# Even superblocks, earlier weight loads, and a PSUM bank for edge weights and sums in a two-layer typed graph transformer

## The chip, the cores and the metric

The kernel runs on one core of one Trainium2 chip. The core has five engines with a queue of instructions each: TensorE (PE, matmuls and transposes by matmul), VectorE (DVE), ScalarE (ACT), GpSimd (POOL) and SyncE (SP), and DMA engines that they feed. The metric is the time of one execution in microseconds (us) on the device.

## The reference, cut to what matters

There are 6,250 nodes with 128 features and 16 types, and 100,000 edges with 32 types, sorted by destination. Each of two layers does:

```python
k = typed_linear(x, ntype, Wk).reshape(n, H, HS)      # H = 8 heads of HS = 16
q = typed_linear(x, ntype, Wq).reshape(n, H, HS)
v = typed_linear(x, ntype, Wv).reshape(n, H, HS)
kT = jnp.einsum('nhd,htdo->nhto', k, Watt)            # every node under every edge type
vT = jnp.einsum('nhd,htdo->nhto', v, Wmsg)
kw = kT[src, :, etype]
m = vT[src, :, etype]
a = jnp.einsum('ehd,ehd->eh', kw, q[dst]) * pri[:, etype].T / SQRT_D
att = edge_softmax(a, dst, n)
hag = jax.ops.segment_sum((m * att[:, :, None]).reshape(-1, H * HS), dst, num_segments=n)
h = jax.nn.silu(typed_linear(hag, ntype, Wa))
alpha = jax.nn.sigmoid(skip[ntype])[:, None]
h = layernorm(h * alpha + x * (1.0 - alpha)) * g + b  # per node
```

Behind the second layer come a linear map (`ff_w`, `ff_b`), the addition of the input and one more layernorm.

## The kernel before

**Tables and gathers.** For every node and every edge type a row of 256 numbers (the key and the value under that edge type) is computed and written to a table in DRAM, one table for each layer (`tabs[0]`, `tabs[1]`). An edge then needs one row of 1 KB, found by its source and type. The nodes are sorted into 49 blocks of 128. Four classes of 11 blocks hold nodes of four types each; five more blocks are mixed and hold any of the 16 types. Within a class the blocks are ordered by degree, and each block has a fixed number of edge slots per node (`OWN_SLOTS` is 25, 21, 19, 18, 17, 16, 15, 15, 14, 12, 11 in each class; the mixed blocks have 28, 20, 16, 14 and 9 gathers). For a slot POOL issues one indirect DMA that gathers 128 rows, one to a partition (L1434), into a buffer `kv` that holds four slots and has 12 copies. Two small memsets into `pause` (L1440) follow every gather on POOL.

**Stages.** From 0 to about 594 us nodes and edges are sorted and the first table is written (98 scatters, L1128). Layer 0 gathers from it until 1888 us. Layer 1 gathers from 1958 to 3106 us, and the last nodes' results leave until 3150 us.

**Superblocks.** Node work is done on superblocks of up to `SB` = 4 consecutive blocks (list `sbs`), 128 to 512 nodes that stand along the free dimension of a tile. The order of the superblocks is the order of the edge work. Before the change a class is cut into its last 3 blocks, its middle 4 and its first 4 by number of blocks alone, and run in the order first, middle, last (83, 63 and 37 slots); mixed superblocks (2 blocks with 48 slots, 3 with 39) follow the first and the second class, and the last class is run as 37, 63, 37 and 46 slots, the last two being pairs of blocks.

**Edge work of a block** (function `edges`). For each buffer of four slots (a chunk), DVE multiplies the keys with the query (L1454, `kv<-kv,q`) and reduces them to one number per slot and head (L1460, `a<-kv`). When a block's gathers are in, the generator `finished` takes over: mask, maximum `m`, difference, exp on ACT, `den` (the sum of the exps), then for each chunk the product of values and weights (`kv<-kv,a`; into `acc` for the first chunk) and the sum into `acc` (`acc<-kv,acc`), and last `sums`, the reduction of the four slots of `acc`. Its instructions go through a recorder, so that all of them have the line L247. In layer 0 weights lie in `a` and sums in `acc`, both in SBUF. In layer 1 the query, the weights and the sums lie in a pair of PSUM banks from the pool `tps` (tile `tb`). One block, `TOP`, has slots for nodes of high degree beside its own; its weights and sums are in SBUF in both layers.

**Node work of a superblock** (generator `nodes`). Sums divided by `den` are transposed (`nb<-ident,hag`), and a typed linear map follows: for each type DVE makes a masked copy `xm` of the transposed features (`xm<-ntb,nb`, or `xm<-ntb,h` where the features have been copied to SBUF first), and PE adds its product with the type's weights in a PSUM bank. Silu, the residual and the layernorm come next. In layer 0 the chain goes on with keys, values and query of the next layer (`wkqv`, outputs `kvT0`, `kvT1` and `qT`, copied out of PSUM by ACT). Then `pieces_of` makes the superblock's part of the second table: for each block and each half of the edge types, matmuls with the edge-type weights `bdk` and `bdv` (L312), copies on ACT (L320, a few on DVE, L318) into `st`, and, eight steps later (`late`, `later`), a scatter on POOL (L1672). In layer 1 the chain ends with the output, scattered by POOL at L1704. The next superblock's query (`queries0`) is made in layer 0 by the same kind of typed map with `wq0`.

**PSUM.** Eight banks: `nps` has two for the node chain (all tiles named `nb`), `tps` three pairs (`tb`).

**What sets the order.** POOL issues in the order in which the code is written. The code is written chunk by chunk, and after each part of a chunk `tick` takes steps of the node work (`work`) and of the table (`pieces`). `spread(work, gen, steps, slots)` says over how many slots so many steps are spread. For the node chain the steps are 33 in layer 0 and 42 in layer 1, more for mixed superblocks (75 in layer 0), and the slots come from `pace`. On DVE, ACT and PE a scheduler orders the instructions, under order dependences that the recorder (`Held`, `stream`) adds so that node work isn't issued sooner than where it was written.

**Start.** `load_later` queues, on SP, the loads of `wq0` and `wa` (1 MB each, L212 and L213), and two memsets on DVE (L511) hold these loads back. DVE scales the keys' edge weights `bdk` by `prit` (L198, L199) before the first table can be computed; SP loads `bdv` and `prit`, ACT loads `bdk`, `Wk` and `Wv`.

## Time and profile before

| what | value |
|---|---|
| median of 3 runs | 3147.55 us (3146.17 to 3155.6) |
| profiled execution | 3152.49 us, span 3150.6 us |
| busy PE / DVE / ACT / POOL | 1561.5 / 1871.8 / 964.4 / 2376.3 us |
| share of the span | 50% / 59% / 31% / 75% |
| gathers of both layers (L1434) | 1,638, mean 998 ns |
| scatters of the second table (L1672) | 98, mean 1062 ns |
| last layer-0 gather to first layer-1 gather | 1887.97 to 1958.36 us |

POOL has the largest share of the span. A row of a view of groups gives busy time and mean, then the engine's idle time ahead of such instructions with what ended it; in the view of waits the columns are total us, times, and the longest. "issue" is idle time in which no wait shows. A window's row gives its length, the busy time of each engine named with its instructions, the granted clock of PE, the share of the 16 DMA engines and GB/s.

### The profile page before, as it was taken

The page shows a single profiled execution, that of the slowest core. Times are in us where ns is not written, and L with a number is a line of the kernel's source. Part 1 is how long each engine was busy: PE and PEld are TensorE (multiplying, and loading weights), DVE is VectorE, ACT ScalarE, POOL GpSimd, SP SyncE. Part 2 cuts the span into 40 slices and gives each one's busy share as a digit, 9 for nine tenths or more (in the row PEclk, how much of TensorE's full clock was granted, in tenths as well). Part 3 has the DMA queues.
Part 4 walks back from the last instruction along what each step waited for, and adds up shares of the span by engine and source line. Part 5 has one row for each costly group of instructions (what it writes and reads, how often), then busy time and mean ns, then how long its engine had stood idle before and what let it go on. Part 6 is the DMA issues. An engine that isn't in the chain of part 4 may idle for free.

```text
span 3150.6 us, 24725 instructions
## 1 busy us (share of the span) xinstructions
PE 1561.5 (50%) x5295; PEld 706.2 (22%) x5295; DVE 1871.8 (59%) x4322; ACT 964.4 (31%) x1599; POOL 2376.3 (75%) x5392
## 2 busy tenths in 40 slices
PE   5999887303675647776688775011221122112112
PEld 2445334101232312332233232000110011001001
DVE  7477655266646656666665553466556675666565
ACT  3887433101444123533354453001100121012111
POOL 3332665588868887888888882888788888888884
PEclk9899766556677767777777686555555556555555
DMA  7999999933777457775688888333333333333331
GB/s 214 421 419 414 390 388 399 299 94 101 256 262 274 157 194 262 279 295 195 233 306 297 304 290 313 104 109 107 99 102 103 110 114 106 100 108 108 98 97 46
DMA packets 174584, 674.80 MB, mean 214 GB/s; under 512 B 52972, under 2 KB 89998, under 8 KB 149374
## 3 DMA queue, kind: packets, MB, share of 16 engines
q0 software_dynamic: 113152, 635.19, 56.1%
q1 hardware_dynamic: 45170, 30.78, 3.4%
q10 hardware_dynamic: 16096, 7.10, 0.9%
q8 instruction: 46, 0.75, 0.1%
q14 instruction: 120, 0.98, 0.1%
HBM read 248.64 MB, written 425.02 MB: 214 GB/s over the span
## 4 chain that ended last, share of the span: by engine, by line
POOL 46%; issue 11%; DMA 10%; DVE 8%; PE 5%; ACT 2%; POOLq 0%; DVEq 0%; ACTq 0%
POOL kv L1434 35%; DMA kv<-tab,ell 9%; POOL pause L1440 7%; PE nb L247 3%; POOL tab L1672 1%; DMA tab<-st,row 1%; DVE kv L1454 1%; POOL out_dram L1704 1%; PE tb L312 1%; DVE kv L247 1%; DVE hs L247 1%; DVE a L1460 1%; DVE acc L247 1%; ACT L247 1%; ACT st L320 1%
## 5 line engine op out<-in xcount | busy, mean ns | idle before, releaser
L1434 POOL DMA_INDIRECT kv<-tab,ell x1638 | 1634.1, 998 | 325.6 <-issue 250.0
L320 ACT COPY st<-tb 128x512 f32<-128x512 f32 (+1 forms) x984 | 677.5, 778 | 555.6 <-PE tb L312 330.4
L1454 DVE TENSOR_TENSOR kv<-kv,tb 128x512 f32<-128x512 f32 (+3 forms) x223 | 143.0, 641 | 449.0 <-DMA kv<-tab,ell 443.6
L1454 DVE TENSOR_TENSOR kv<-kv,q 128x512 f32<-128x512 f32 (+3 forms) x223 | 143.6, 645 | 410.5 <-DMA kv<-tab,ell 404.1
L247 PE MATMUL nb<-ident,hag 128*128 128x128 f32 x98 | 27.1, 417 | 722.2 <-DVE hag L247 722.1
L1440 POOL MEMSET pause<- 128x32 bf16 x3276 | 334.2, 142 | 0.7
L312 PE MATMUL tb<-bdv,kvT 32*128 32x512 f32 x784 | 259.4, 799 | 52.3 <-ACT st L320 51.7
L312 PE MATMUL tb<-bdv,vT 32*128 32x512 f32 x784 | 260.2, 784 | 48.8 <-ACT st L320 45.0
L1460 DVE TENSOR_REDUCE a<-kv 128x32 f32<-128x512 f32 (+2 forms) x446 | 281.5, 634 | 1.2
L1128 POOL DMA_INDIRECT tab<-st,rows x98 | 101.6, 1037 | 199.5 <-ACT st L320 165.3
L247 PE MATMUL nb<-xm,wa 128*128 128x512 f32 (+2 forms) x336 | 187.3, 715 | 106.0 <-DVE xm L247 105.8
L312 PE MATMUL tb<-bdk,kvT 32*128 32x512 f32 x784 | 231.9, 776 | 14.1 <-ACT st L320 13.7
L247 PE MATMUL nb<-xm,wkqv 128*128 128x384 f32 (+2 forms) x504 | 209.5, 579 | 20.8 <-DVE xm L247 20.8
L318 DVE COPY st<-tb 128x512 f32<-128x512 f32 (+1 forms) x192 | 128.7, 708 | 147.6 <-PE tb L312 78.3
L312 PE MATMUL tb<-bdk,kT 32*128 32x512 f32 x784 | 206.0, 783 | 6.5 <-issue 5.8
L247 PEld LDWEIGHTS nb<-ident,hag 128*128 128x128 f32 x98 | 16.1, 205 | 740.5 <-issue 510.5
L247 DVE SCALAR_TENSOR_TENSOR xm<-ntb,nb 128x512 f32<-128x512 bf16 (+2 forms) x304 | 155.3, 562 | 40.0 <-PE nb L247 39.8
L247 PE MATMUL nb<-xm,wq 128*128 128x384 f32 (+2 forms) x168 | 88.5, 678 | 163.4 <-DVE xm L247 163.4
L1672 POOL DMA_INDIRECT tab<-st,row x98 | 104.1, 1062 | 83.7 <-ACT st L320 59.9
L247 PEld LDWEIGHTS nb<-xm,wkqv 128*128 128x128 f32 x504 | 111.7, 228 | 126.0 <-issue 45.5
L247 DVE TENSOR_TENSOR tb<-kv,tb 128x512 f32<-128x512 f32 (+3 forms) x216 | 138.6, 642 | 0.2
L247 PE MATMUL nb<-ident,hs 128*128 128x128 f32 x98 | 33.5, 469 | 205.6 <-DVE hs L247 198.4
(342 smaller groups left out, 2467.8 us busy)
## 6 DMA issues: line engine op xcount, KB each, us to landing
kv<-tab,ell POOLq DMA_INDIRECT x1638
hr<-xrd SPq DMA_DIRECT2D x14, 256.0 KB
hqd<-hs SPq DMA_DIRECT2D x7, 512.0 KB, 3.1
hq<-hqd SPq DMA_DIRECT2D x7, 512.0 KB
xrd<-xr SPq DMA_DIRECT2D x10, 256.0 KB, 23.2
hr<-xrd SPq DMA_DIRECT2D x10, 192.0 KB, 2.8
hqd<-hs SPq DMA_DIRECT2D x5, 384.0 KB
hq<-hqd SPq DMA_DIRECT2D x5, 384.0 KB, 3.2
```

The costliest lines, as they stand in the source:

```text
L247: put = issue(*args, **kwargs)
L312: stream[nc.tensor] = nc.tensor.matmul(pt[:, b], yT[s, i * P:(i + 1) * P], bd[s, tt, :], start=True, stop=True)
L318: nc.vector.tensor_copy(to, pt)
L320: stream[nc.scalar] = nc.scalar.copy(to, pt)
L1128: put = nc.gpsimd.indirect_dma_start(out=tabs[0].rearrange("(n t) c -> n (t c)", t=16), out_offset=bass.IndirectOffsetOnAxis(ap=rows1[:, t ...
L1434: get = nc.gpsimd.indirect_dma_start(out=kv[:, j - j0, :], out_offset=None, in_=tabs[l][:], in_offset=bass.IndirectOffsetOnAxis(ap=ell[:, ...
L1440: nc.gpsimd.memset(pause[:, at % PAUSES, half], 0.0)
L1454: stream[nc.vector] = nc.vector.tensor_tensor(kk, kk, of.unsqueeze(1).to_broadcast([P, c, D]), op=ALU.mult)
L1460: nc.vector.tensor_reduce(to, kk.rearrange("p k (h d) -> p k h d", h=H), axis=AX.X, op=ALU.add)
L1672: put = nc.gpsimd.indirect_dma_start(out=tabs[1].rearrange("(n t) c -> n (t c)", t=16), out_offset=bass.IndirectOffsetOnAxis(ap=row2[:, tg ...
L1704: put = nc.gpsimd.indirect_dma_start(out=out, out_offset=bass.IndirectOffsetOnAxis(ap=node[:, b:b + 1], axis=0), in_=o[:, i, :], in_offset ...
```

## The change

1. The loads of `wq0` and `wa` go to SP directly behind the load of the edge types; the two memsets on DVE that held them go away.
2. Superblocks of a class are cut so that the largest number of slots is as small as can be: `superblocks_of_slots` gives blocks 0 to 2 (65 slots), 3 to 6 (66) and 7 to 10 (52), run in the order 66, 52, 65; the last class is run as blocks 7 to 10 (52), 4 to 6 (48), and then the two pairs of 37 and 46 slots that it ended with before (its first two superblocks had 37 and 63).
3. The slots over which node work is spread come from `room` and `asking` instead of `pace`, mixed superblocks have 91 steps in layer 0 instead of 75, and the table pieces of the last four superblocks are spread over one slot less.
4. In layer 0 a block's weights and sums lie in one PSUM bank (`hold`), sums two slots wide instead of four. A chunk's product is one instruction as before (two in the first chunk), its sum two instructions of 256 numbers a partition. `TOP` keeps SBUF.
5. That bank comes from `nps`, which has one bank left. `linear_of` asks for its output only when the masked copies are made, since features and output share the bank; with 16 types it first copies the features to SBUF (`h2`). The `wkqv` maps of a mixed superblock run in three passes, one for each output, instead of two, and for the other superblocks the matmuls of an output are issued two types at a time.

Core of the diff:

```diff
     def load_later():
-        nc.sync.dma_start(wq0, Wq[0].rearrange("t d o -> d t o"))
-        nc.sync.dma_start(wa, Wa[0].rearrange("t d o -> d t o"))
...
     nc.sync.dma_start(eti, etype)
+    nc.sync.dma_start(wq0, Wq[0].rearrange("t d o -> d t o"))
+    nc.sync.dma_start(wa, Wa[0].rearrange("t d o -> d t o"))
...
-    for w in (wq0, wa):
-        nc.vector.memset(w[:, 0, 0:1], 0.0)
...
+    def linear_of(pool, nps, types, ntb, hT, n, w):
+        types = list(types)
+        if len(types) > TC:
+            h2 = pool.tile([P, SB * P], F32, name="h2", tag="hb")
+            on.scalar.copy(h2[:, :n], hT[:, :n])
+            yield
+            hT = h2
+        some, ps = 2 if len(types) > TC else TC, None
+        for t0 in range(0, len(types), some):
+            xms = list(masked(pool, types[t0:t0 + some], ntb, hT, n))
+            yield
+            if ps is None:
+                ps = nps.tile([P, SB * P], F32, name="nb")
+            for t, xm in xms:
+                on.tensor.matmul(ps[:, :n], w[:, t, :], xm[:, :n],
+                                 start=(t == types[0]), stop=(t == types[-1]))
+            if t != types[-1]:
+                yield
+        return ps
...
-        nps = ctx2.enter_context(tc.tile_pool(name="nps", bufs=2 if fast else 5, space=PSUM))
+        nps = ctx2.enter_context(tc.tile_pool(name="nps", bufs=1 if fast else 5, space=PSUM))
+        hold_ps = ctx2.enter_context(tc.tile_pool(name="hold", bufs=1, space=PSUM)) if fast else None
...
+            evenly = sorted(superblocks_of_slots(OWN_SLOTS),
+                            key=lambda at: sum(OWN_SLOTS[at[0]:at[0] + at[1]]))
             for c in range(NC):
-                cut = [(CB - i0 - k, k) for i0, k in reversed(list(superblocks(CB)))]
+                cut = [evenly[-1], *evenly[:-1]]
                 if c == NC - 1:
-                    cut = [(CB - i0 - k, k) for i0, k in superblocks(CB - SB)]
+                    cut = [(i0 + SB, k) for i0, k in
+                           reversed(superblocks_of_slots(OWN_SLOTS[SB:]))]
                     cut += [(i0, 2) for i0 in range(SB - 2, -1, -2)]
...
                 w = av
-                if l and rest is None:
-                    w = pair[:, 1, D:D + K * H].rearrange("p (k h) -> p k h", h=H)
+                if rest is None:
+                    if l == 0:
+                        held = hold_ps.tile([P, SB * P], F32, name="hold")
+                    w = (pair[:, 1, D:D + K * H] if l else held[:, 2 * D:2 * D + K * H]).rearrange(
+                        "p (k h) -> p k h", h=H)
                 on.scalar.activation(w, av, AF.Exp)
...
-                if l == 0 or rest is not None:
+                if rest is not None:
                     acc = ep.tile([P, CH, D], F32, name="acc", bufs=1)
+                elif l:
+                    acc = pair[:, 0].rearrange("p (k c) -> p k c", k=CH)
                 else:
-                    acc = pair[:, 0].rearrange("p (k c) -> p k c", k=CH)
+                    acc = held[:, :2 * D].rearrange("p (k c) -> p k c", k=2)
+                wide = acc.shape[1]
...
-                    if j > 1:
+                    if j:
                         j0, j1 = chunks[j - 1]
-                        on.vector.tensor_tensor(acc[:, :j1 - j0], kvt[j - 1][:, :j1 - j0, D:],
-                                                acc[:, :j1 - j0], op=ALU.add)
+                        for c0 in range(0 if j > 1 else wide, j1 - j0, wide):
+                            c = min(wide, j1 - j0 - c0)
+                            on.vector.tensor_tensor(acc[:, :c], kvt[j - 1][:, c0:c0 + c, D:],
+                                                    acc[:, :c], op=ALU.add)
...
-                           (42 if l else 33) + (0 if len(sbs[s][2]) == TC else 14 if l else 42),
-                           pace(s + 1) * (1.0 if l or mixed(s) else 0.75))
+                           (42 if l else 33) + (0 if len(sbs[s][2]) == TC else 14 if l else 58),
+                           room(s))
...
+            def asking(s):
+                if l == 0 and mixed(s + 1):
+                    return 26
+                return 0.5 * GB[sbs[s][0]]
+
+            def room(s):
+                then = min(s + 1, len(sbs) - 1)
+                if l or mixed(s):
+                    return slots(then) - 0.5 * GB[sbs[then][0]]
+                if s + 2 >= len(sbs):
+                    return 0.75 * (slots(then) - 0.5 * GB[sbs[then][0]])
+                return slots(then) - max(18, asking(then)) + 8
...
-                    for js in ((0, 1), (2,)):
+                    for j in range(3):
...
                             on.tensor.matmul(ps[:, :n], wkqv[:, j, t, :], xm[:, :n],
                                              start=(t == types[0]), stop=(t == types[-1]))
-                        yield
+                            if t % 2:
+                                yield
```

Where the instructions stand on the engines, before and after:

On SP at the start of the program, before the change; names are the tiles above, and a row's bracket names the counters that it waits for (`DMAHW` are those of DMA lanes that SP and ACT share):

```order
L341 DMA eti<-in_edge_type_dram 128x782
L191 DMA bdv<-in_L_gnn_Wmsg_dram 16x32x16 [waits DVE_49]
L193 DMA prit<-in_L_gnn_pri_dram 16x32 [waits DMAHW0_49]
...
L720 DMA kvs<-kvi 128x782 [waits DMAHW0_49,DVE_49]
L212 DMA wq_90<-in_L_gnn_Wq_dram 128x16x128 [waits DMAHW1_49]
L213 DMA wa<-in_L_gnn_Wa_dram 128x16x128 [waits DMAHW2_49]
```

and after it:

```order
L380 DMA eti<-in_edge_type_dram 128x782
L381 DMA wq_90<-in_L_gnn_Wq_dram 128x16x128
L382 DMA wa<-in_L_gnn_Wa_dram 128x16x128 [waits DMAHW1_49]
L191 DMA bdv<-in_L_gnn_Wmsg_dram 16x32x16 [waits DMAHW4_49,DVE_49]
L193 DMA prit<-in_L_gnn_pri_dram 16x32 [waits DMAHW6_49]
```

Both weight loads stand ahead of the `bdv` and `prit` loads instead of behind them and behind the store of `kvs`.

On DVE in layer 0, where one of the first blocks is finished, before the change:

```order
L247 TENSOR_REDUCE den<-a 128x8 [waits Activation_49]
L247 TENSOR_TENSOR acc<-kv,a 128x512
L247 TENSOR_TENSOR kv<-kv,a 128x4x128
L1460 TENSOR_REDUCE a<-kv 128x32 [waits DVE_49]
L247 TENSOR_TENSOR kv<-kv,a 128x4x128
L247 TENSOR_TENSOR acc<-kv,acc 128x512 [waits DVE_49]
```

and after it (the recorder's line is now L264), with the end of that block and the start of the next one's sums:

```order
L264 TENSOR_REDUCE den<-hold 128x8 [waits Activation_49]
L1530 TENSOR_REDUCE a<-kv 128x32 [waits DVE_49]
L264 TENSOR_TENSOR hold<-kv,hold 128x256 [waits DVE_49]
L1524 TENSOR_TENSOR kv<-kv,q 128x4x128 [waits DMASW2_49,DMASW7_49,DMASW1_49,DMASW0_49]
L264 TENSOR_TENSOR kv<-kv,hold 128x2x128 [waits DVE_49]
...
L264 TENSOR_REDUCE sums<-hold 128x128 [waits DVE_49]
L1524 TENSOR_TENSOR kv<-kv,q 128x4x128 [waits DMASW2_49,DMASW3_49,DMASW1_49,DMASW0_49]
L264 TENSOR_REDUCE den<-hold 128x8 [waits Activation_49]
```

Weights and sums are read from `hold`, the first chunk's product is cut in two, and between one block's `sums` and the next one's `den`, for which ACT must have written the bank anew, stands one product with the query.

On PE in layer 0, at the first superblock's maps to keys, values and query and the first table matmuls, before the change:

```order
L247 MATMUL nb<-xm,wkqv 128x512 [waits DMAHW1_49,DVE_49]
...
L247 MATMUL nb<-xm,wkqv 128x512 [waits DMAHW0_49,PE_49]
...
L247 MATMUL nb<-xm,wkqv 128x512 [waits DMAHW2_49,Activation_49]
...
L312 MATMUL tb<-bdk,kvT_6679 128x512 [waits DMAHW6_49,DMAHW3_49]
L247 MATMUL nb<-ident,qT 128x128 [waits Activation_49]
```

and after it:

```order
L264 MATMUL nb<-xm,wkqv 128x512 [waits DMAHW1_49,DVE_49,PE_49]
...
L264 MATMUL nb<-xm,wkqv 128x512 [waits DMAHW0_49,Activation_49]
...
L351 MATMUL tb<-bdk,kvT_6637 128x512 [waits DMAHW6_49,DMAHW3_49]
L264 MATMUL nb<-xm,wkqv 128x512 [waits DMAHW2_49,Activation_49]
...
L351 MATMUL tb<-bdk,kvT_6637 128x512 [waits DMAHW4_49,DMAHW1_49]
L264 MATMUL nb<-ident,qT 128x128 [waits Activation_49]
```

The second output's matmuls now wait for ACT's copy too, and a table matmul stands between the second and the third.

60 lines of the change are left out of this document (36 added, 24 removed).

## The prediction

> **What bounds the kernel now.** I read the page's first parts, then the waits of POOL, then POOL's gathers by layer, and last what stands beside a slow gather. Columns of a timeline row: start, duration, engine, line, operation, tiles, and in brackets the idle time before it with what ended it.
>
> ```profile
> span 3150.6 us, 24725 instructions
> POOL 3332665588868887888888882888788888888884
> POOL 46%; issue 11%; DMA 10%; DVE 8%; PE 5%; ACT 2%; POOLq 0%; DVEq 0%; ACTq 0%
> ```
>
> From slice 9 to the end POOL is busy 8 tenths, and the chain that ended last is mostly POOL. POOL issues the 1,638 gathers (L1434), two pacing memsets (L1440) behind each, and the scatters of the second table (L1672). What remains idle in a slot is a fixed 0.15 us of issue, so a slot lasts 0.95 + 0.15 + 0.20 + about 0.01 us = 1.31 us and the layers last as long as POOL's queue. A microsecond counts if POOL stops for it, or if a gather itself takes longer. Both are visible in layer 0:
>
> ```profile
> 594.00:1990.00 1396.00, 871.30 (x844) 0.72 0.68 239
> 1990.00:3106.00 1116.00, 762.77 (x795) 0.54 0.35 104
> L1434 POOL DMA_INDIRECT kv<-tab,ell x844: 952/952/3714, 594.1 to 1989.8; - x169
> L1434 POOL DMA_INDIRECT kv<-tab,ell x795: 951/952/2406, 1989.8 to 3104.8; - x199
> ```
>
> Rows 1 and 2 are POOL's busy time in gathers by window, rows 3 and 4 their minimum, median and maximum in ns. Median 952 in both layers, yet layer 0 has 871.30 - 844 x 0.952 = 67.8 us above it, layer 1 only 762.77 - 795 x 0.952 = 5.9. The layers do the same gathers; they differ in where DVE's operands lie. Layer 0 keeps weights (a) and sums (acc) in SBUF, layer 1 in PSUM (tb). Beside the slowest gather:
>
> ```profile
> 1145.99 0.68 DVE L1454 TENSOR_TENSOR kv<-kv,q 128x512 f32<-128x512 f32 x1
> 1146.17 1.93 POOL L1434 DMA_INDIRECT kv<-tab,ell  x1 [0.15 <-issue]
> 1148.39 0.68 DVE L247 TENSOR_TENSOR acc<-kv,acc 128x512 f32<-128x512 f32 x1
> 1148.45 3.71 POOL L1434 DMA_INDIRECT kv<-tab,ell  x1 [0.15 <-issue]
> 1148.99 0.68 DVE L247 TENSOR_TENSOR kv<-kv,a 128x512 f32<-128x512 f32 x1
> 1150.66 0.68 DVE L247 TENSOR_TENSOR acc<-kv,acc 128x512 f32<-128x512 f32 x1
> 1152.52 0.95 POOL L1434 DMA_INDIRECT kv<-tab,ell  x1 [0.15 <-issue]
> 1885.22 1.44 POOL L1434 DMA_INDIRECT kv<-tab,ell  x1 [0.15 <-issue]
> 1415.56 2.18 POOL L1434 DMA_INDIRECT kv<-tab,ell  x1 [0.15 <-DMA tab<-st,row]
> ```
>
> The gather of 1148.45 lasts until DVE's run of products and sums with two SBUF inputs is over. I laid each of layer 0's 189 gathers above 1.00 us beside the DVE instructions it overlaps: 118 (the first at 643.88 with 1.00 us, the last at 1885.22) overlap a product with a or a sum into acc, 45.5 us above the median; 17 overlap mostly xm<-ntb,h, which also reads twice from SBUF (1415.56 is one), 5.3 us; the remaining 54 overlap kv<-kv,q and others, 15.3 us.
>
> The second loss is POOL standing still:
>
> ```profile
> POOL tab L1672 <- ACT st L320: 59.9, 10, 22.7
> POOL kv L1434 <- DVE acc L247: 20.6, 9, 11.6
> 879.71 1.01 POOL L1672 DMA_INDIRECT tab<-st,row  x1 [8.05 <-ACT st L320]
> 942.54 1.18 POOL L1434 DMA_INDIRECT kv<-tab,ell  x1 [11.56 <-DVE acc L247]
> 1234.47 1.01 POOL L1672 DMA_INDIRECT tab<-st,row  x1 [4.88 <-ACT st L320]
> 1261.91 1.48 POOL L1672 DMA_INDIRECT tab<-st,row  x1 [8.50 <-ACT st L320]
> ```
>
> Those four amount to 33.0 us in the middle of layer 0. Behind the one of 942.54 stands a long piece of PE:
>
> ```profile
> 929.46 7.61 PE L247 MATMUL nb<-xm,wkqv 128*128 128x384 f32 x21
> 940.38 0.51 ACT L247 ACTIVATE a<-a 128x336 f32<-128x336 f32 x1
> 940.92 0.76 DVE L247 TENSOR_REDUCE den<-a 128x8 f32<-128x336 f32 x1 [7.71 <-ACT a L247]
> ```
>
> ACT's exp stands in its queue behind copies of PE's outputs; DVE waits 7.71 us for it, the 12 gather buffers stay full, POOL waits 11.56.
>
> **The change part by part.**
>
> *Weight loads earlier.* Two 1 MB loads leave the middle of the preparation:
>
> ```profile
> 36.14 0.85 SPq L212 DMA_DIRECT2D wq<-in_L_gnn_Wq_dram  x1
> 37.45 2.68 SPq L213 DMA_DIRECT2D wa<-in_L_gnn_Wa_dram  x1
> 40.00:44.00 4.00, 0.16 (x1) 0.00 (x0) 0.00 (x0) 0.30 (x2) 0.45 (x1) 1.00 1.05 300
> 45.92 2.04 PE L312 MATMUL tb<-bdk,kT 32*128 32x512 f32 x5 [5.76 <-issue]
> ```
>
> From 40 to 44 us the DMA engines are full (share 1.05) while PE does 0.16 us, and the first table matmul starts 5.76 us late. Without the loads I take -4.5, some of the wait being the node-row gathers'. They now go ahead of the bdv and prit loads, which shift back; two memsets vanish, and the loads take other DMA lanes, on which bdk's loads wait. If prit, which DVE needs, comes later than that wait saved, the end is +4; if all goes, -7.
>
> *Weights and sums in PSUM.* The 118 gathers' cause goes, except in the one block with overflow edges (SBUF still) and beside what is left in SBUF: 45.5 - 4.5 = -41. Ends: 0 (kv<-kv,q takes the place) and -45.5. DVE pays:
>
> ```profile
> L247 DVE TENSOR_TENSOR kv<-kv,a 128x512 f32<-128x512 f32 x135 | 90.9, 683 | 0.0
> L247 DVE TENSOR_TENSOR kv<-kv,tb 128x512 f32<-128x512 f32 x130 | 86.2, 678 | 0.1
> L247 DVE TENSOR_TENSOR acc<-kv,acc 128x256 f32<-128x256 f32 x10 | 4.2, 417 | 0.0
> L247 DVE TENSOR_REDUCE sums<-acc 128x128 f32<-128x512 f32 x49 | 50.7, 1034 | 0.0
> L247 DVE SCALAR_TENSOR_TENSOR xm<-ntb,h 128x384 f32<-128x384 bf16 x32 | 16.7, 554 | 3.2 <-PE nb L247 2.7 <-ACT h L247 0.3
> 594.00:1958.00 1364.00, 865.97 (x2710) 363.37 (x2710) 813.74 (x1758) 492.34 (x663) 1116.93 (x2555) 0.72 0.68 242
> 1360.00:1440.00 80.00, 65.40 (x197) 29.91 (x197) 59.30 (x126) 23.63 (x34) 70.66 (x156) 0.83 0.63 225
> ```
>
> The product costs the same (678 against 683 ns). The sum is two instructions of 256 wide: 2 x 417 - 684 = 150 ns more for each of 135 + 49 chunks (the first chunk's product is also cut in two), 27 us; the reduction reads 256 instead of 512, about half of 1034, -25. Estimate +2 to +20 us of DVE in all. The third window column is DVE: 813.74 of 1364 us, 60%, so this hides; if it did not, it would be the +20. A new wait: the bank is one, so exp of a block waits until the block before is reduced, and behind it in ACT's queue wait table copies, behind den the sums. At most a copy and an exp, about 1.5 us, 48 times, on DVE's idle 550 us: nothing. [...]
>
> *One bank for the node chain.* In the two superblocks of all 16 types, xm now reads h2 from SBUF everywhere: from 64 such instructions in layer 0 to 160 (query 32, after-attention 32, and wkqv in three passes instead of two, 96), at 5.3 / 64 = 0.083 us of gather each: 96 x 0.083 = +8. In layer 1, 32 more: +2.7. Ends: 0 and double. The added pass is 32 xm x about 0.5 = 16 us of DVE, 8 in each mixed stretch: 59.30 becomes some 70 of 80 us, still under POOL's pace. PE waits at each wkqv output until ACT has copied the one before: a copy as short as exp's 0.51 and what is queued ahead of it. I allow 2.4 us a wait, under a third of the 7.71 that den waited for ACT's queue, three times a chain, 7 us. Scatters are issued 8 steps late (about 12 slots of 1.31 us, 16 us), which absorbs it. At a layer's end nothing does, but ACT's queue is short there: one such wait, +2.4 in layer 0 and +2 in layer 1.
>
> *Even superblocks and the planner's numbers.* Largest superblock 83 slots before, 66 after; node work is told to use more of the superblock behind it (58 steps instead of 42 for mixed), and the matmuls of 4 types come two at a time, so exp stands behind less. I take off 23 of the 33.0 us; all or nothing are the ends, and as much as 22 can come anew in the mixed stretches.
>
> *End of layer 0.*
>
> ```profile
> 1888.34 1.02 POOL L1672 DMA_INDIRECT tab<-st,row  x1 [0.17 <-issue]
> 1933.10 0.97 POOL L1672 DMA_INDIRECT tab<-st,row  x1 [22.72 <-ACT st L320]
> 1958.36 0.99 POOL L1434 DMA_INDIRECT kv<-tab,ell  x1 [11.99 <-DMA tab<-st,row]
> ```
>
> From the last gather (1887.97) to layer 1 are 70 us, its chain: finish, node chain, table, landing. The last superblock is the same two blocks; the order shows 8 scatters behind the last gather instead of 10, -2, against the +2.4: 0.
>
> **Sum.** -4.5 - 41 + 8 - 23 + 0 + 2.7 + 2 = -55.8. The profiled execution took 3152.49 us (1.9 around its span), 4.9 above the median of 3147.55; the difference is set against the median: 3092. 0.3% is 9.4 us, about what a measurement of this kernel can tell from no change.
>
> **The rivals.**
>
> *Stalls stay or move.* The gathers are cured but the mixed stretches fill DVE, and exp still stands behind copies. For it: 59.30 of 80 us already, more work there. Against: longer room for the node work. Without the 23: 3115; with 20 new: 3135.
>
> *kv<-kv,q takes the place.* It keeps two SBUF inputs:
>
> ```profile
> L1454 DVE TENSOR_TENSOR kv<-kv,q 128x512 f32<-128x512 f32 x184 | 127.0, 691 | 369.8 <-DMA kv<-tab,ell 364.8 <-issue 4.7
> ```
>
> For it: 15.3 us are beside it and others today. Against: it comes singly, paced by landings (its idle time, 369.8 us, ends with DMA), and has 127.0 us beside the others' 215 or so (products 90.9, as many sums of 684 ns, 49 first products), but at most 15.3 us of the excess beside their 45.5. Half the gain lost: 3113.
>
> *Operands aren't the cause.* Then only DVE's run, not its inputs, holds POOL: none of -41 + 8, so 3125. Against: layer 1 runs the same sequence from PSUM with 5.9 us. [...]
>
> *Slower: the one bank.* PE is in order; a matmul that waits for ACT's copy holds table matmuls queued behind it, ACT holds exp, and POOL the scatter. It decides when a chain is late by the 16 us of slack and 4.7 more in each of the 14 node chains (66 us, to above 3157). Against: the three waits make 7 us.
>
> **Chances.** Forecast 0.55 (alone 3075 to 3108), stalls 0.20, kv<-kv,q 0.09, operands 0.05, the one bank 0.11. Of the stalls and operands 0.04 ends within 9.4 us of before, of the bank 0.01; so faster 0.85, same 0.05, slower 0.10. Low: everything gone, -7 - 45.5 + 5 - 33 = -80, with the +4.7, 3070, some lower for fewer stalls in layer 1 (3063); high 3138 takes in the first three rivals.
>
> **What would show it.** Right: some 840 us instead of 871.30 for layer 0's 844 gathers, median 952; the four waits under 10 us together; PE's idle before the first table matmul near 1 us; xm<-ntb,h 160 in layer 0, slow gathers only there. Wrong: gathers' total unchanged, POOL waiting for DVE's hold or st in the mixed stretches, PE idle at nb released by ACT with scatters late behind.

## The result, and the profile after

The changed kernel takes 3120.59 us (median of 4 runs, 3117.41 to 3121.85), the kernel before 3151.57 us (4 runs). The ratio is 0.9891 with a 95% interval of 0.9871 to 0.9912: 1.1% faster, some 31 us where 56 were forecast.

The profiled execution took 3117.41 us. From the page of the changed kernel, the span, POOL in 40 slices, and the chain that ended last by engine:

```profile
span 3115.6 us, 25058 instructions
POOL 3332665488888888888888864888788888888884
POOL 41%; DVE 11%; issue 10%; DMA 10%; PE 6%; ACT 2%; POOLq 0%; DVEq 0%; ACTq 0%
```

POOL still sets the pace; the dip in slices 24 and 25 is the stretch between the layers. Its gathers (now L1504), layer 0's 819 by window and by minimum, median and maximum, then layer 1's 819:

```profile
594.00:1843.00 1249.00, 805.28 (x819) 0.75 0.70 247
L1504 POOL DMA_INDIRECT kv<-tab,ell x819: 952/952/3987, 594.7 to 1841.4; - x164
L1504 POOL DMA_INDIRECT kv<-tab,ell x819: 951/952/4115, 1916.3 to 3068.1; - x164
```

For the same 819 gathers the kernel before has these rows:

```profile
594.00:1890.00 1296.00, 848.22 (x819) 0.73 0.68 237
L1434 POOL DMA_INDIRECT kv<-tab,ell x819: 952/952/3714, 594.1 to 1887.0; - x164
L1434 POOL DMA_INDIRECT kv<-tab,ell x819: 951/952/2406, 1958.4 to 3104.8; - x164
```

The median gather is unchanged and layer 0's are 42.9 us shorter in sum: the excess over 952 ns fell from 68.5 to 25.6 us. First and last start in these rows cut the span into five stretches:

| stretch (us) | before | after | difference |
|---|---|---|---|
| up to the first gather of layer 0 | 594.1 | 594.7 | +0.6 |
| first to last gather of layer 0 | 1292.9 | 1246.7 | -46.2 |
| last gather of layer 0 to first of layer 1 | 71.4 | 74.9 | +3.5 |
| first to last gather of layer 1 | 1146.4 | 1151.8 | +5.4 |
| from there to the end | 45.8 | 47.5 | +1.7 |

Everything gained lies in layer 0's gathering, and the other four stretches give back 11 us. POOL's longest stops in layer 0, the counterparts of the four of before:

```profile
791.33 1.14 POOL L1740 DMA_INDIRECT tab<-st,row  x1 [3.56 <-ACT st L359]
924.54 1.25 POOL L1504 DMA_INDIRECT kv<-tab,ell  x1 [6.70 <-DVE t L264]
1153.55 1.31 POOL L1740 DMA_INDIRECT tab<-st,row  x1 [5.17 <-ACT st L359]
1329.98 1.16 POOL L1740 DMA_INDIRECT tab<-st,row  x1 [3.58 <-ACT hold L264]
```

They are shorter but more: ten stops of over 1 us with 28.2 us in all, against four with 33.0. The one at 924.54 stands at the block with overflow edges (`TOP`), as the one of 11.56 us at 942.54 did before. DVE's groups in layer 0 that answer to those shown of before:

```profile
L264 DVE TENSOR_TENSOR hold<-kv,hold 128x256 f32<-128x256 f32 x381 | 160.7, 422 | 3.8
L264 DVE TENSOR_TENSOR kv<-kv,hold 128x512 f32<-128x512 f32 x130 | 88.4, 680 | 1.0
L264 DVE SCALAR_TENSOR_TENSOR xm<-ntb,h 128x384 f32<-128x384 bf16 x80 | 42.3, 553 | 11.3 <-PE nb L264 6.6 <-ACT h L264 3.9
L264 DVE TENSOR_REDUCE sums<-hold 128x128 f32<-128x256 f32 x48 | 19.9, 415 | 0.5
594.00:1916.00 1322.00, 843.11 (x2710) 350.10 (x2710) 837.84 (x2032) 492.99 (x660) 1072.65 (x2555) 0.75 0.70 249
```

The last row is the window of layer 0 up to layer 1 (third column DVE): 837.84 us instead of 813.74, in 42 us less.

### The profile page after: what moved, and what is told of

It reads as the page before. It is cut to its first block, busy times and chain, and to the rows that moved or that the text cites. A ratio compares the mean times of both kernels' runs of the same rounds, so it can differ in the third digit from the quotient of the medians.

```text
span 3115.6 us, 25058 instructions
## 1 busy us (share of the span) xinstructions
PE 1542.5 (50%) x5295; PEld 692.5 (22%) x5295; DVE 1896.9 (61%) x4594; ACT 966.2 (31%) x1605; POOL 2335.1 (75%) x5392
## 4 chain that ended last, share of the span: by engine, by line
POOL 41%; DVE 11%; issue 10%; DMA 10%; PE 6%; ACT 2%; POOLq 0%; DVEq 0%; ACTq 0%
POOL kv L1504 32%; DMA kv<-tab,ell 8%; POOL pause L1510 7%; PE nb L264 5%; DMA tab<-st,row 2%; DVE xm L264 2%; PE tb L351 2%; DVE kv L264 1%; DVE kv L1524 1%; POOL out_dram L1772 1%; DVE hold L264 1%; DVE hs L264 1%; DVE a L1530 1%; POOL tab L1740 1%; ACT L264 1%
## 5 line engine op out<-in xcount | busy, mean ns | idle before, releaser
L1504 POOL DMA_INDIRECT kv<-tab,ell x1638 | 1593.7, 973 | 324.7 <-issue 247.2
L264 PE MATMUL nb<-ident,hag 128*128 128x128 f32 x98 | 26.2, 406 | 641.7 <-DVE hag L264 613.1
L1530 DVE TENSOR_REDUCE a<-kv 128x32 f32<-128x512 f32 (+3 forms) x446 | 281.3, 633 | 1.3
L264 PE MATMUL nb<-xm,wa 128*128 128x384 f32 (+2 forms) x336 | 188.8, 726 | 150.1 <-DVE xm L264 145.2
L264 PE MATMUL nb<-xm,wkqv 128*128 128x384 f32 (+2 forms) x504 | 217.9, 582 | 55.1 <-DVE xm L264 44.3
L351 PE MATMUL tb<-bdv,kvT 32*128 32x512 f32 x784 | 223.2, 749 | 42.5 <-ACT st L359 42.1
L351 PE MATMUL tb<-bdk,kT 32*128 32x512 f32 x784 | 212.3, 809 | 1.9 <-DMA kvs<-kvi 1.9
L264 DVE TENSOR_TENSOR hold<-kv,hold 128x256 f32<-128x256 f32 (+1 forms) x410 | 169.1, 412 | 4.2
L264 PEld LDWEIGHTS nb<-ident,hag 128*128 128x128 f32 x98 | 15.5, 200 | 660.8 <-issue 459.5
L264 PE MATMUL nb<-xm,wq 128*128 128x384 f32 (+2 forms) x168 | 87.0, 672 | 136.3 <-DVE xm L264 130.2
L264 PEld LDWEIGHTS nb<-xm,wa 128*128 128x128 f32 x336 | 89.6, 283 | 250.5 <-issue 190.5
L264 PEld LDWEIGHTS nb<-xm,wkqv 128*128 128x128 f32 x504 | 106.0, 223 | 175.8 <-issue 94.5
L264 DVE TENSOR_TENSOR tb<-kv,tb 128x512 f32<-128x512 f32 (+3 forms) x216 | 138.5, 641 | 0.2
```

The costliest lines, as they stand in the source:

```text
L264: put = issue(*args, **kwargs)
L351: stream[nc.tensor] = nc.tensor.matmul(pt[:, b], yT[s, i * P:(i + 1) * P], bd[s, tt, :], start=True, stop=True)
L1504: get = nc.gpsimd.indirect_dma_start(out=kv[:, j - j0, :], out_offset=None, in_=tabs[l][:], in_offset=bass.IndirectOffsetOnAxis(ap=ell[:, ...
L1530: nc.vector.tensor_reduce(to, kk.rearrange("p k (h d) -> p k h d", h=H), axis=AX.X, op=ALU.add)
```

## The experiments

Twelve runs followed, on three chips; e5 and e6 are the changed kernel and the kernel before once more, e10 and e12 repeat e1 and e3. On two of them the kernel before takes 3149 to 3156 us, as in the first measurement (e5 to e8, e11 and e12 on one, e9 and e10 on the other). On the third, where e1 to e4 ran, it takes 3340. Each ratio is to the kernel before, measured beside it on the same chip. "Stops" are POOL's idle times of over 1 us between the first and the last gather of layer 0, added up from its timeline; the excess is that of layer 0's 819 gathers over 952 ns each. Where a part of it is given, the gathers of over 1 us are divided by the DVE instructions that they overlap.

| run | median us | ratio, 95% interval | excess | stops |
|---|---|---|---|---|
| e1 sums in SBUF (slow chip) | 3352.6 | 1.0028 (1.0005 to 1.0051) | 88.1 | 100.4 |
| e2 only acc in SBUF (slow chip) | 3346.5 | 1.0007 (0.9981 to 1.0033) | 47.7 | 148.5 |
| e3 old superblocks (slow chip) | 3394.0 | 1.0175 (1.0138 to 1.0211) | 26.5 | 194.8 |
| e4 loads back (slow chip) | 3363.5 | 1.0077 (1.005 to 1.0104) | 34.3 | 157.2 |
| e5 the changed kernel | 3123.7 | 0.9888 (0.9872 to 0.9905) | 32.7 | 27.4 |
| e6 the kernel before, one run | 3158.7 | | 78.5 | 32.4 |
| e7 superblocks alone | 3150.8 | 0.9979 (0.9962 to 0.9996) | 82.1 | 12.7 |
| e8 second bank when free | 3114.4 | 0.9859 (0.9842 to 0.9875) | 31.8 | 28.3 |
| e9 e8, loads at layer 0 | 3107.5 | 0.9862 (0.9837 to 0.9887) | 29.6 | 28.4 |
| e10 e1 again | 3181.4 | 1.0096 (1.0073 to 1.0119) | 88.1 | 29.0 |
| e11 banks 2, 2, 2 pairs | 3125.2 | 0.9912 (0.9879 to 0.9946) | 35.7 | 18.6 |
| e12 e3 again | 3143.8 | 0.9957 (0.9942 to 0.9973) | 39.2 | 41.5 |

Two traces of one kernel differ in excess by up to 13 us (e3 and e12; the kernel before has 68.5 and 78.5, the changed kernel 25.6 and 32.7), so a few us of excess between two runs show nothing. Their stops agree within 1 us on the chips that aren't slow (33.0 and 32.4, 28.2 and 27.4).

**e1 and e10: weights and sums back in SBUF.** The edit to the changed kernel, of which the removal of the pool `hold` is left out:

```diff
-                if rest is None:
-                    if l == 0:
-                        held = hold_ps.tile([P, SB * P], F32, name="hold")
-                    w = (pair[:, 1, D:D + K * H] if l else held[:, 2 * D:2 * D + K * H]).rearrange(
-                        "p (k h) -> p k h", h=H)
+                if l and rest is None:
+                    w = pair[:, 1, D:D + K * H].rearrange("p (k h) -> p k h", h=H)
...
-                if rest is not None:
+                if l == 0 or rest is not None:
                     acc = ep.tile([P, CH, D], F32, name="acc", bufs=1)
-                elif l:
+                else:
                     acc = pair[:, 0].rearrange("p (k c) -> p k c", k=CH)
-                else:
-                    acc = held[:, :2 * D].rearrange("p (k c) -> p k c", k=2)
```

Expected of the first run:

> The changed kernel with layer 0's weights in a and its sums in acc, four slots wide, both in SBUF again; the node chain keeps its one bank, the eighth bank lies unused. Theory (two SBUF inputs on DVE hold up the gathers): layer 0's excess of its 819 gathers over 952 ns returns from 25.6 to 62 to 75 us, most of it beside kv<-kv,a and acc<-kv,acc, and the time rises by 35 to 50 us over the changed kernel, to 3155 to 3170. Rival (the excess fell because the new superblocks and the cut sums spread DVE's work): the excess stays under 40 us and the time within 15 us of the changed kernel.

and of the second:

> The kernel of e1 once more, hoped for on a chip like the first. It has the even superblocks and the one bank of the node chain, but not the bank of weights and sums. Stops of over 1 us in layer 0 are 12.7 us with the superblocks alone (e7) and 27.4 with everything (e5). If the one bank of the node chain makes the 15 us more: 24 to 30 here. If the bank of weights and sums makes them (exp of a block waits until the block before is reduced, and ACT's copies wait behind it): 10 to 16 here. Excess of layer 0's gathers 75 to 90 us in either case, time 3155 to 3175.

Layer 0's gathers in e10, and those of the changed kernel in e5:

```profile
594.00:1911.00 1317.00, 867.76 (x819) 0.73 0.67 235
593.00:1850.00 1257.00, 812.35 (x819) 0.73 0.70 245
```

The excess returned on both chips, to 88.1 us, 61.7 and 64.7 of it beside products with a and sums into acc (121 gathers in e10; 3 in e5). On e10's own chip e9, which keeps the bank, has 29.6 us. So the two-SBUF-input theory holds against the rival, which wanted it to stay under 40. The edit also makes the sums four slots wide again, but the width isn't the cause: layer 1 of e10 makes sums as wide in PSUM, and the excess of its 819 gathers is 8.4 us. In time the bank of weights and sums is worth more than forecast: 3181.4 us without it (3155 to 3175 were expected) on a chip where the kernel before takes 3149, against 3123.7 with it where that takes 3156. And it makes no stops there: e10 has 29.0 us of them without it, e5 has 27.4 with it. The largest of e10's:

```profile
938.10 1.25 POOL L1498 DMA_INDIRECT kv<-tab,ell  x1 [6.13 <-DVE t L264]
1459.09 1.02 POOL L1734 DMA_INDIRECT tab<-st,row  x1 [7.17 <-ACT st L359]
```

The first of these stands in the first mixed superblock, the second 150 us behind the other one. So the expectation's first branch is the right one: the stops come with the node chain as it is written for one bank, not with the bank of weights and sums.

**e2: only acc in SBUF.** The second of e1's two edits alone.

> The changed kernel with only the sums moved back to SBUF (acc, four slots wide); the weights stay in the PSUM bank. So the product has one SBUF input and the sum has two. Theory of two SBUF inputs, each instruction by itself: about half of the lost excess returns, 20 of 42 us (excess 40 to 52), beside acc<-kv,acc alone. Rival (only an unbroken run of such instructions holds up a gather): a product from PSUM between two sums lets the gather finish, and the excess stays under 32 us.

The excess is 47.7 us, as the theory wants (40 to 52): 20.3 of it beside sums into acc (51 gathers), a third of e1's 61.7. So an unbroken run of instructions with two SBUF inputs isn't needed; sums alone, with products between them that have one operand in PSUM, do harm. The sums are 109 of the 252 us that such instructions take on DVE in e1, more than two fifths, so a run of products and sums seems to cost more than its parts; products alone weren't tried.

**e3 and e12: the old cut of the superblocks and the old spreading numbers in the changed kernel.**

```diff
-                cut = [evenly[-1], *evenly[:-1]]
+                cut = [(CB - i0 - k, k) for i0, k in reversed(list(superblocks(CB)))]
                 if c == NC - 1:
-                    cut = [(i0 + SB, k) for i0, k in
-                           reversed(superblocks_of_slots(OWN_SLOTS[SB:]))]
+                    cut = [(CB - i0 - k, k) for i0, k in superblocks(CB - SB)]
...
-                           room(s))
+                           pace(s + 1) * (1.0 if l or mixed(s) else 0.75))
```

> The changed kernel with the old cut of the superblocks and the old numbers for spreading node work and table pieces; everything else as changed. If even superblocks are worth what the traces show (POOL's stops of over 1 us in layer 0: 33.0 us before, 28.2 after), the time is 0 to 10 us above the changed kernel. My prediction's step (they take off 23 us): 20 us or more above it, with stops of 45 us or more. If the one bank needs the even cut, since the mixed superblocks' three passes have too little room without it, 15 to 40 us above, with stops at the mixed superblocks.

> The kernel of e3 (the changed kernel with the old cut and the old spreading numbers) once more, hoped for on a chip like the first. If the parts add up: the superblocks took 19.7 us of stops (e6 to e7), the one bank brought 15 (e7 to e10), so the old cut with the banks has 32.4 + 15 = 47 us of stops in layer 0, and layer 1 and its end are back at 1147 and 45.9 us: time 10 to 15 us over the changed kernel. If the three passes over 16 types had too little room in the old cut: stops of 60 us or more, mostly at the mixed superblocks, time 30 us or more over.

On the slow chip e3 is the slowest of the four kernels, with the most stops (194.8 us). e12 takes 20 us more than e5 on the same chip, between its two branches, with 41.5 us of stops instead of 27.4, 4 us more between the layers and 6.5 us more excess. Its largest stops stand in the two mixed superblocks (853 to 942 and 1218 to 1287 us), where before's stood, and just behind the second:

```profile
936.21 1.16 POOL L1508 DMA_INDIRECT kv<-tab,ell  x1 [12.70 <-DVE acc L264]
1260.45 1.02 POOL L1744 DMA_INDIRECT tab<-st,row  x1 [6.51 <-ACT st L359]
1305.97 1.02 POOL L1744 DMA_INDIRECT tab<-st,row  x1 [6.17 <-ACT st L359]
```

The parts add up roughly (47 us of stops were expected), and the even cut is worth its 20 us in the presence of the banks. Layer 1 was expected back at 1147 us and was at 1152.3, so it is longer with the old cut too.

**e4: the loads back in their old place.** The hunks of the diff on `load_later`, the loads behind `eti` and the memsets are undone.

> The changed kernel with the loads of wq0 and wa back in load_later behind the two memsets. By the traces the earlier place won nothing (first table matmul at 45.92 us before and 47.62 after, first gather of layer 0 at 594.1 and 594.7): first table matmul at 45.5 to 46.5, first gather 0 to 2 us earlier, time within 4 us of the changed kernel. By my prediction's step the time rises by 4.5 us.

In its trace the first table matmul stands at 40.9 us and the first gather at 588.3; e1 to e3 on the same chip, with the early loads, have 46.4 to 47.3 and 593.7 to 593.9. The early place costs 5.5 us there, where I had expected 0 to 2. The time can't say so, since the changed kernel itself has not run on that chip.

**e5 and e6: both kernels again on one chip.**

> The changed kernel itself. The runs e1 to e4 came from a chip on which the kernel before takes 3340 us instead of 3150; layer 1, which the change hardly touches, takes 1235 us there instead of 1150. Theory: that chip adds stops to POOL's queue (idle time in layer 1 170 us instead of 85) and the parts of the change keep their worth: the time is 25 to 40 us under the kernel before on the same chip, and 35 to 50 us under e1 if it is the chip of e1. Rival: with so much idle time more the gain is gone, since POOL waits for the table's scatters in layer 0 (28.2 us of stops on the first chip, over 100 in e1 and e4): within 10 us of the kernel before.

> The kernel before, for a trace from the chip of this call. If it is a chip like that of e1 to e4: layer 1 about 1235 us with idle time of about 170 us, gathers of layer 0 with the same excess as on the first chip (60 to 75 us over 952 ns), and the stops of POOL in layer 0 well above 33 us. The theory that the excess comes from DVE's operands wants it the same on each chip.

Both ran on a chip like the first, and repeat the first comparison: a ratio of 0.9888, gathers of layer 0 858.2 to 812.3 us (excess 78.5 to 32.7), stops 32.4 to 27.4. What the change gives on the slow chip stays open.

**e7: even superblocks and their numbers alone**, put into the kernel before (that part of the diff, with 42 steps more for mixed superblocks).

> The kernel before with the even superblocks and the planner's new numbers alone (42 steps more for mixed superblocks as before, since their maps keep two passes): no bank for weights and sums, two banks for the node chain, the loads where they were. By the traces the cut took 0 to 10 us off: time 0 to 12 us under the kernel before on the same chip, stops of over 1 us in layer 0 20 to 33 us on a chip like the first. By my prediction 23 us under it. Against e1, which has the one bank of the node chain and the early loads beside it: the difference is what the one bank costs, by my prediction 11 us with 8 of it gathers beside xm<-ntb,h, by the traces about 5.

Stops fall from 32.4 to 12.7 us. Only three are left, none of them in a mixed superblock or just behind one:

```profile
789.96 1.27 POOL L1706 DMA_INDIRECT tab<-st,row  x1 [5.23 <-ACT st L339]
1163.03 1.02 POOL L1706 DMA_INDIRECT tab<-st,row  x1 [5.43 <-ACT st L339]
1166.09 1.32 POOL L1468 DMA_INDIRECT kv<-tab,ell  x1 [2.04 <-DVE xm L266]
```

This is close to the 23 us of my prediction; by the traces I had come to expect 0 to 12. The time falls by 5 us only: layer 0's gathering is 9.9 us shorter (its gathers take 3.6 us more and the scatters among them 6.4), but layer 1 takes 1152.8 us instead of 1147.3, with a stop of 11.4 instead of 7.8 at the block with overflow, and its end 47.5 instead of 45.9. Against e10, which adds the one bank's node chain and the early loads, stops go from 12.7 to 29.0: the chain's price in layer 0 is 16 us of stops, where none were forecast. The excess goes from 82.1 to 88.1; these 6 us, of 8 forecast, are less than two traces of one kernel differ by.

**e8: the bank of weights and sums as the node chain's second bank where it is free**, in layer 1 and for layer 0's last superblock.

```diff
+        class Two:
+            n = 0
+            def tile(self, shape, dtype, name):
+                self.n += 1
+                if self.n % 2:
+                    return nps.tile(shape, dtype, name=name)
+                return hold_ps.tile(shape, dtype, name="hold")
+        two = Two() if fast else nps
...
+            free = last or final
+            nps = two if free else one
...
-            y = yield from linear_of(npl, nps, types, ntb, hT, n, wa)
+            if free:
+                y = nps.tile([P, SB * P], F32, name="nb")
+                yield from linear_steps(npl, types, ntb, hT, n, [(y, wa)])
+            else:
+                y = yield from linear_of(npl, nps, types, ntb, hT, n, wa)
```

> The changed kernel with the bank of weights and sums used as the node chain's second bank where it is free: in layer 1, and for the last superblock of layer 0. If the one bank is what cost time there (layer 1 1151.8 us instead of 1146.4, its end 47.5 instead of 45.9, the stretch between the layers 74.9 instead of 71.3), layer 1 is 3 to 6 us shorter, its end 1 to 2, the stretch between the layers 1 to 3: 5 to 10 us under the changed kernel on the same chip. Rival: layer 1's difference is one stop beside the block with overflow (11.1 instead of 7.7 us) and the stretch between the layers waits for the last gather's landing: under 3 us in all.

Against e5 the stretch between the layers falls from 74.1 to 70.7 us, layer 1 from 1153.4 to 1150.7, its end from 47.2 to 45.7: 7.6 us, and 9.3 in the medians. The theory holds in size. But `linear_steps` also leaves out the copy of the features to SBUF (layer 1's 32 `xm<-ntb,h` become `xm<-ntb,hold`), and layer 1's excess falls from 10.6 to 7.6 us, as much as layer 1 itself; so there the gain may be that of operands, and not of a wait for the bank. It isn't the whole of layer 1: e7 has two banks there too and 1152.8 us, and the stop at the overflow block stays at 11.4 us in e8.

**e9: e8, with the loads of wq0 and wa at the start of layer 0.**

```diff
-    nc.sync.dma_start(wq0, Wq[0].rearrange("t d o -> d t o"))
-    nc.sync.dma_start(wa, Wa[0].rearrange("t d o -> d t o"))
...
     def arm(fast):
+        nc.sync.dma_start(wq0, Wq[0].rearrange("t d o -> d t o"))
+        nc.sync.dma_start(wa, Wa[0].rearrange("t d o -> d t o"))
```

> As e8 (the free bank used as the node chain's second bank), and the loads of wq0 and wa queued on SP at the start of layer 0, where they are first wanted, instead of ahead of the edge weights. In the traces with the early loads (e1, e2, e3, e5, e8) the first table matmul stands at 46.3 to 47.3 us and the node rows' first gather lands at 42 to 43.6; with the loads behind the node rows' gathers (before, e4, e6, e7) the rows are there at 37.5 to 38.1, the matmul follows at 40.9 to 45.9. Theory: without any of these loads by then the first matmul stands at 40 to 41.5, the first gather of layer 0 is 4 to 6 us earlier than e8's 593.5, and the time 3 to 6 us under e8's 3114 on a chip like its. Rival: the first query waits for wq0's landing at the start of layer 0, and what the start wins is lost there: within 2 us of e8.

From the windows of the start (columns PE, weight loads, DVE, ACT, POOL, clock, DMA share, GB/s), the stretch from 36 to 40 us in the changed kernel and in e9:

```profile
36.00:40.00 4.00, 0.00 (x0) 0.00 (x0) 0.00 (x0) 0.00 (x0) 3.09 (x4) 1.00 0.73 54
36.00:40.00 4.00, 1.67 (x5) 1.11 (x5) 0.00 (x0) 0.57 (x3) 3.09 (x4) 1.00 0.44 141
```

The first table matmul stands at 41.3 us and the first gather at 589.9; on the same chip e10, with the early loads, has 46.6 and 594.9. The start wins 5 us, and nothing is lost at layer 0. With 3107.5 us e9 is the fastest kernel measured, 42 us under the kernel before on its chip; relative to that it can't be told from e8 (0.9862 and 0.9859).

**e11: the banks dealt out as two for the chain, two for weights and sums, two pairs for the table.** The edit is the three pools' `bufs`: 2, 2 and 2 instead of 1, 1 and 3.

> The changed kernel with the eight banks dealt out otherwise: two for the node chain, two for weights and sums, two pairs instead of three for the table's matmuls (and layer 1's blocks). Stops of over 1 us in layer 0 were 12.7 us with the superblocks alone and two banks for the chain (e7), 27.4 with everything (e5), 29.0 with one bank for the chain and no bank for the sums (e10). Theory (the one bank of the chain makes them): stops at the mixed superblocks, at about 925 and 1330 to 1420 us, go, 10 to 16 us less. Against it stands the price of the third pair: PE waits for ACT's copy of a table bank more often, the table after the last gather takes longer (stretch between the layers 74 to 85 instead of 74.1). Time from 10 us under to 10 us over the changed kernel; if table scatters come late all over layer 0, 20 or more over.

Stops fall to 18.6 us and layer 0's gathering to 1246.0 from e5's 1254.4. But the table behind the last gather, with two pairs, takes 83.5 us instead of 74.1, and POOL waits 5 to 6 us for seven of the last eight scatters:

```profile
1901.23 0.97 POOL L1740 DMA_INDIRECT tab<-st,row  x1 [5.83 <-DVE st L357]
1908.09 0.97 POOL L1740 DMA_INDIRECT tab<-st,row  x1 [5.88 <-DVE st L357]
```

The time is that of e5, 3125.2 against 3123.7 us. But the stops that went are not those expected. Gone are the ones ahead of the mixed superblocks (5.3 us at 792 and 3.9 at 1156 in e5), which e7 has too. In the first mixed superblock and behind both, e5 has 6.1 + 2.4 + 1.2 + 4.2 + 1.3 + 1.9 = 17.1 us of stops and e11 still 3.4 + 2.1 + 1.5 + 2.1 + 2.4 + 2.8 = 14.3 (its other 4.3 stand ahead of the last gather), where e7 has none. So a second bank alone doesn't undo them; what e11 keeps of the change is the code written for one bank, the features in SBUF, the three passes over 16 types and their 91 steps. Which of these makes the stops wasn't tried.

## Why the prediction was right, point by point

The direction, the time (3120.6 in 3063 to 3138) and the main mechanism, the gathers, were right. The time lies outside the likeliest case's own range of 3075 to 3108, since the sum was too hopeful by 21 us (55.8 against the 35.0 between the two traces); the whole range held because it was wide enough for three rivals. Of the signs named ahead, the shorter gathers (by 42.9 us where some 31 were forecast), the 160 xm<-ntb,h and PE's short wait (1.94 us) came. "The four waits under 10 us together" did not, and POOL waiting for st about the mixed superblocks, a sign of being wrong, did. One reading was off without effect: the window of 844 gathers reached 25 gathers into layer 1, and layer 0's own 819 have 68.5 us above the median instead of 67.8. And the +5 in the low end has no term behind it. By the terms of the sum:

- **Weights and sums in PSUM, -41.** Right. The 118 gathers beside such instructions, 45.5 us, became 3 with 3.7 us, all about the block that keeps SBUF: -41.8. One is this row of the changed kernel, beside its products with a and sums into acc:

```profile
927.46 3.99 POOL L1504 DMA_INDIRECT kv<-tab,ell  x1 [0.16 <-issue]
```

- **kv<-kv,q taking the place** (a rival): no. 12.8 us before, 9.8 after. **Operands not the cause** (a rival): e1, e2 and e10 exclude it (an excess of 88.1, 47.7 and 88.1 us, against 25.6 and 32.7 with weights and sums in the bank), with layer 1 beside them. e10 and e5 differ by 55.4 us of gathers (867.76 against 812.35) with tensor_tensor's operands. But two SBUF inputs aren't the whole of it: kv<-kv,q, which has them as well, does much less harm, 12.8 us in 144 us of DVE before, the products and sums 45.5 in 251. By what path such an instruction holds up a gather was not shown.
- **DVE's price, hidden.** Right: 24 us more in layer 0 (837.84 against 813.74), within the +2 to +20 of the bank and the 16 of the third pass. From 1360 to 1440 us DVE is busy 65.06 us, where I had some 70. The product takes 680 ns with its weights in hold, 683 with them in a, so the bank costs that instruction nothing.
- **xm<-ntb,h, +8 in layer 0 and +2.7 in layer 1.** Too dear: 160 instead of 64 of them, with 7.1 us instead of 5.3 in the first pair of traces (12.6 instead of 6.9 in e5 and e6), and 1.0 in layer 1. By luck, this hides a part of the misses below.
- **Weight loads, -4.5.** Wrong, the step failed. I costed the loads where they were and not what they push back. The changed kernel's start on SP and POOL:

```profile
4.74 6.39 SPq L382 DMA_DIRECT2D wa<-in_L_gnn_Wa_dram  x1
11.24 6.45 SPq L191 DMA_DIRECT2D bdv<-in_L_gnn_Wmsg_dram  x1
28.60 0.48 SPq L193 DMA_DIRECT2D prit<-in_L_gnn_pri_dram  x1
30.60 2.96 SPq L763 DMA_DIRECT2D tab<-zeros  x6
29.15 1.59 POOL L517 DMA_INDIRECT xg<-in_x_dram,inv  x1 [23.86 <-DVE inv L500]
```

  SP stands at the second load and at the one behind it for 6.4 us each, and the last of the many small loads of bdv and prit is issued 7.6 us later than before (28.60 against 20.99). So they and the zeros come together with the first gather of node rows, whose landing lets PE begin (its weight load at 43.63 us waited 11.58 for it). That gather is issued as before (29.15 against 29.17), but PE starts at 43.66 us instead of 38.14, and in 36 to 40 us the DMA engines are busy 0.73 with 54 GB/s. That the small transfers delay the landing is inferred from this. The wait that I wanted to remove did shrink (5.76 to 1.94 us), behind a longer one. Taking the loads out of their old place is worth at most what I forecast (e9, with neither place, has its first table matmul at 41.3 us; the old place gives 40.9, 42.2, 45.5 and 45.92 in e4, e7, e6 and before). What the early place costs against the old one varies: layer 0's first gather stands at 588.3, 590.0, 592.2 and 594.1 us with the old place (e4, e7, e6, before), and at 593.5 to 595.0 in the nine traces with the early one.
- **Even superblocks, -23.** Right alone in stops (e7: 19.7 us), though the time fell by 5 us only there; right in time beside the banks (e12: 20 us). In the sum it is hidden: together with the one bank only 4.8 us of stops went.
- **One bank for the node chain: PE's waits and the third pass absorbed.** Wrong, this is the largest miss. I held 7 us of waits a chain against a slack of 16, and DVE's 70 us against 80 in a mixed stretch, and booked nothing. e7 and e10 show 16 us of new stops. PE and ACT behind the second mixed superblock, in the changed kernel:

```profile
1318.29 4.54 PE L264 MATMUL nb<-xm,wa 128*128 128x384 f32 x8 [1.21 <-DVE xm L264]
1322.76 1.13 PE L351 MATMUL tb<-bdk,kvT 32*128 32x512 f32 x4
1323.94 1.01 ACT L359 COPY st<-tb 128x1024 f32<-128x1024 f32 x1 [5.38 <-PE tb L351]
```

  The superblock's map over 16 types stands ahead of the table's matmuls on PE; ACT waits 5.38 us for them, and POOL 3.58 for the scatter at 1329.98. The stop at 987.45, behind the first one, looks alike: ACT's copy waits 3.82 us for table matmuls behind others of wa. The largest stop, 6.70 us at the block with overflow, is of another kind, since it is what is left of before's 11.56; e7 has none there. I priced the chain's mean delay in every superblock, and not the 16-type chain, which has the most to do and the least room, by itself. Which part of the new code makes the stops stays open (e11).
- **End of layer 0, 0.** Off by 3.5, and by 5.3 between e6 and e5. e8, which gives this chain its second bank back, takes 3.4 off. Another part is the last gather: the last product with the query begins 8.5 us after that gather's issue instead of 5.4, and 8.2 after it in e8.
- **Layer 1, +4.7.** 7.1 measured. e8, with the second bank and without the copy of the features, takes 4.2 off; for the rest, with the longer stop at the overflow block, e7 and e12 point both to the cut and to the banks. This isn't settled.

The rival of stalls that stay or move, at 3115 to 3135, is what came out: the old ones went or shrank, and some 16 us of others came with the one bank's chain. It had expected DVE to fill up. The queue that shows in the rows is PE's, table matmuls behind the node chain, which is the slower rival's mechanism at a quarter of its price.

## What to carry to other kernels

A gather that POOL issues while DVE runs instructions with two SBUF inputs can take almost four times as long (3.71 us instead of 0.95 in this kernel); compare the sum of the gathers with count times median, and move one of DVE's operands to PSUM where that excess is on the path. When a change takes a PSUM bank from one chain for another, price the poorer chain at its longest stage, with the code that it now needs, and give it the bank back wherever the other has no use for it. And a load that is moved ahead can be paid by what queues behind it (here the last load of prit was issued 7.6 us later, and PE began 5.5 us later): follow the queue to the first landing that an engine waits for.

## What the runs showed of the hardware

On one of three chips POOL, DVE, ACT and PE stand still at odd moments without a wait that the profile explains; it puts such idle time down to "remote" or "issue" (in e4 "remote" ends 97.8 us of the idle time ahead of ACT's copies into st, 75.4 ahead of DVE's xm, 32.5 ahead of POOL's pauses and 11.7 ahead of PE's nb; in the changed kernel on the first chip, none). In e4, groups of POOL's instructions from 2030 to 3060 us, almost all of it in layer 1, with the idle time ahead of them, and those of the changed kernel on the first chip:

```profile
L1513 POOL MEMSET pause<- 128x32 bf16 x1324 | 136.3, 141 | 41.9 <-remote 23.2 <-issue 15.9 <-POOL pause L1513 0.5
```

```profile
L1510 POOL MEMSET pause<- 128x32 bf16 x1452 | 148.0, 141 | 0.5
```

The changed kernel's 1,452 memsets have 0.5 us of idle time ahead of them, the 1,324 there 41.9. The instructions themselves take the same 141 ns. Layer 1 lasts 1235 us instead of 1150, and the kernel before 3340 instead of 3150. No part that was tried on this chip (e1 to e4) is faster than the kernel before, although e4's gathers have as little excess as on the others; POOL waits for the table's copies instead (e4):

```profile
POOL tab L1743 <- ACT st L361: 100.5, 28, 9.6
POOL tab L1743 <- ACT hold L266: 28.9, 9, 5.5
```

In e5, on a chip without such pauses, the first of these rows is 27.3 us. Why that chip pauses wasn't found out. The runs there show that what POOL saves in gathers comes back as stops: the excess is 88.1, 47.7 and 34.3 us in e1, e2 and e4, the stops 100.4, 148.5 and 157.2, and the sum of both 188.5, 196.2 and 191.5.
